# A state-space layer on one Trainium2 core: the first of two output products goes directly behind the projections, into another PSUM bank, and one column is copied ahead of the gating

## The chip, the cores and the metric

The kernel runs on one core of one Trainium2 chip. The metric is device time in microseconds (us) of one execution. Times of the kernel before: 1736.02, 1733.81 and 1731.57 us, median 1733.81.

## The reference

The input has 4 images of 128 channels and 96 x 96 pixels. The reference normalizes it in 32 groups of channels, reads it as four sequences of 9216 positions (rows forward, rows in reverse, columns forward, columns in reverse), runs the same scan layer on each, fuses the four results with a 1x1 convolution and adds the input. All is float32. The scan layer, cut to what matters here:

```python
t = _grouped1x1(x, in_proj_w, in_proj_b, G)
u, gate = (t[:, :HID], t[:, HID:])          # HID = 256
u = jax.nn.silu(u)
u = conv_general_dilated(u, dw_w, ..., feature_group_count=HID)   # 5 taps
s = _conv1x1(u, ssm_in_w)                   # 32 channels
a = DMIN + (DMAX - DMIN) * sigmoid(_conv1x1(u, ssm_delta_w, ssm_delta_b))
bb = tanh(_conv1x1(u, ssm_b_w, ssm_b_b))
cc = tanh(_conv1x1(u, ssm_c_w, ssm_c_b))
hst = ...                                   # h[l] = a[l] * h[l-1] + bb[l] * s[l]
u = u + _conv1x1(cc * hst + ssm_d[None, :, None] * s, ssm_out_w)
u = _grouped1x1(u * sigmoid(gate), mix_w, mix_b, G)
return _conv1x1(u, out_proj_w, out_proj_b)
```

## The kernel before, in words

**Tiling.** The program makes 8 passes over an image: for each of the 4 images one over columns (V) and one over rows (H). A pass takes the forward and the reverse sequence together. It has 6 steps of 4 *pairs*; a pair is one of four interleaved phases of a step, 384 positions of the forward unit (s = 0) and 384 of the reverse unit (s = 1). That makes 192 pairs, t = 0 to 191; k = t % 4 is the pair's place in its step. A helper `pair` issues the first 6 pairs, `pair_on` (L1038) those from t = 6 to 191, and `tail` the rest. The order of all instructions is the order in which the code issues them; no scheduler changes it. Each engine works through its own queue in order. In the text PE is the matrix engine, DVE the vector engine, ACT the scalar engine, POOL GpSimd, and SP the queue that issues transfers.

**A pair.** `pair_on(t)` does the front part of pair t and the back part of pair n = t - 6, whose recurrence is done by then. `bi` is the first unit of pair n. In the order of the code:

- *under(bi, 1)* (L659, the copy at L662): ACT copies u of the reverse unit into PSUM, two banks at a time, as the start value onto which ssm_out is added. The banks are given by `ssm`: 0 and 1 for the forward unit, 2 and 3 for the reverse one.
- *taps* (L814, L828): the upper half of the channels. The first tap is made by ACT a pair ahead (`first_tap`, L826); the four others are one DVE instruction each, the last writing u. They work in banks 0 and 1, which are also the forward unit's ssm_out banks.
- *band* (`conv`, L724): the lower half of the channels, 8 matmuls with a banded weight into banks 6 and 7. Phases k = 0 and 1 need a second part, *less* (`conv_less`, L784), and then ACT copies the banks into u (`copy_u`, L801); here these are called double pairs. In phases k = 2 and 3, the single pairs, DVE adds a row from the tile `lone` instead (`add_lone`, L775).
- *recurrence(t)* and *stats_chunks(t)*: DVE's scan (only k = 0 and 1), POOL's products for the scan's output, and in some pairs two blocks of statistics for the next image on DVE (L436).
- *first output product* (`add_next(w[0])`, `accumulate` at L931): 8 matmuls with the fused output weight w_fin on the gated u of the forward unit of pair n - 1, into bank 4. Then ACT copies the bank into ys (L946; L944 adds a bias in the last half of the H passes), and POOL adds ys to the output in SBUF (L963). The add is held back into the next pair where k = 3.
- *less* (double pairs), *under(bi, 0)*, *copy_u* (double pairs), and the *second output product* of the reverse unit into bank 5, again with a ys copy and a POOL add.
- *gates and ssm_out*: four matmuls for the gate of a later pair (L630) or the input projection of a later step (L492), into banks 4, 7, 6 and 5, mixed with the four matmuls of ssm_out (`out_of`, L650).
- *gating* (L700, the operation at L711): DVE multiplies ssm_out's result with the gate into u, in place, first the forward unit, then the reverse one. Between the two, the code hands ACT two activations on banks 4 and 5 (L505, L666 or L672).
- `first_tap(i + 2)` on ACT, then an activation on banks 6 and 7 (L516 or L672), and transfers.
- *proj* (L840): 16 matmuls of the projections with the weight `main` into banks 4 and 5; ACT's tanh tm (L865), copy (L868) and tanh (L874); POOL's start of the scan input; and `scale_s` (L886) on ACT.

A matmul of 128 x 32 weights fills a quarter of the array, so four of them run side by side. The trace has two MATMUL records for each float32 matmul.

**Waits.** An instruction waits for one semaphore itself. What else it waits for stands in separate wait instructions right ahead of it on the same engine.

## Time and profile before

| | |
|---|---|
| median of the three runs | 1733.81 us |
| the profiled execution's own time | 1736.02 us |
| its span, first to last instruction | 1734.3 us |
| matmuls (PE) busy | 1706.6 us |
| DVE busy | 1506.4 us |
| ACT busy | 1479.8 us |
| POOL busy | 1478.3 us |
| granted TensorE clock, mean | 0.998 |

The profile is one of the three runs. PE stands for matmuls and PEld for weight loads, which overlap them. In a timeline row the numbers are the start from the span's beginning and the length; rows of equal instructions that follow each other are merged, with their count. Brackets hold the idle time of the engine ahead of the row and what ended it. A line number can be that of a helper: L131 issues every matmul of proj, band, less and the output products, which are told apart by their weights (main, band, less, w_fin).

### The profile page before, as it was taken

Reading aid. Unit: us, or ns where it says so; the run is one execution under the profiler, and the core shown is the slowest. Engines: PE = TensorE matmul, PEld = TensorE weight load, DVE = VectorE, ACT = ScalarE, POOL = GpSimd, SP = SyncE. Lnnn points to the kernel's source line nnn. Section 1 sums busy time; section 2 is a strip of 40 time slices with the busy share of each in tenths; the row PEclk is TensorE's granted clock in tenths of the full one; section 3 lists DMA queues with packets and bytes.
Section 4 is the critical chain, followed back from the end, with each engine's and each line's share of the span. In section 5 each row is a group of like instructions: output and inputs, shape, how many; then the busy total and the mean of one; then the engine's idle time right before and its main releaser. Section 6 shows DMA issues by size and latency. Waiting matters only on the chain.

```text
span 1734.3 us, 50199 instructions
## 1 busy us (share of the span) xinstructions
PE 1706.6 (98%) x20410; PEld 703.5 (41%) x20410; DVE 1506.4 (87%) x1508; ACT 1479.8 (85%) x2435; POOL 1478.3 (85%) x1455
## 2 busy tenths in 40 slices
PE   7999999999999999999999999999999999999998
PEld 3343344434443434444444434444344433444333
DVE  6799998888889999888888989988888888888897
ACT  4788888888888888888888888888888888888875
POOL 3589898888889988988888988989888889998887
PEclk9999999999999999999999999999999999999999
DMA  7755885358994788337797488733899538753474
GB/s 241 208 169 163 281 242 146 131 197 261 287 289 152 232 245 246 124 132 251 238 306 232 154 275 239 216 117 126 253 287 288 192 119 275 227 167 116 132 239 169
DMA packets 143140, 362.63 MB, mean 209 GB/s; under 512 B 19264, under 2 KB 85696, under 8 KB 142912
## 3 DMA queue, kind: packets, MB, share of 16 engines
q1 hardware_dynamic: 142768, 359.39, 66.7%
q8 instruction: 162, 2.65, 0.7%
q14 instruction: 66, 0.54, 0.1%
q10 hardware_dynamic: 144, 0.04, 0.0%
HBM read 197.77 MB, written 126.70 MB: 187 GB/s over the span
## 4 chain that ended last, share of the span: by engine, by line
PE 89%; DMA 4%; DVE 3%; ACT 2%; issue 1%; POOL 0%; SPq 0%; ACTq 0%; DVEq 0%; POOLq 0%
PE psum L131 72%; PE psum L650 6%; PE psum L630 5%; PE psum L492 5%; DMA kept<-shared 2%; DVE psum L828 1%; DMA sil<-shared 1%; DMA sil<-sil 1%; DVE t L903 1%; DVE u L711 1%; ACT psum L826 1%; DMA acc<-in_xr 0%; PE psum L1274 0%; ACT psum L662 0%; ACT shared L516 0%
## 5 line engine op out<-in xcount | busy, mean ns | idle before, releaser
L828 DVE SCALAR_TENSOR_TENSOR psum<-sil,small,psum 128x768 f32<-128x768 f32 x576 | 589.2, 1023 | 51.6 <-ACT psum L826 34.0
L131 PE MATMUL psum<-u,w_fin 128*32 128x384 f32 (+1 forms) x6192 | 554.6, 485 | 1.1 <-ACT ys L944 0.5
L131 PE MATMUL psum<-u,main 128*32 128x384 f32 x6144 | 537.1, 490 | 1.2 <-ACT shared L672 0.6
L711 DVE SCALAR_TENSOR_TENSOR u<-gate,psum 128x768 f32<-128x768 f32 x376 | 341.9, 951 | 137.9 <-PE psum L650 65.0
L963 POOL TENSOR_TENSOR acc<-ys,acc 128x384 f32<-128x384 f32 x375 | 441.5, 1199 | 12.5 <-ACT ys L944 1.9
L131 PEld LDWEIGHTS psum<-u,w_fin 128*32 128x32 f32 x6192 | 203.1, 109 | 307.9 <-issue 209.3
L131 PEld LDWEIGHTS psum<-u,main 128*32 128x32 f32 x6144 | 180.2, 110 | 328.7 <-issue 207.3
L662 ACT COPY psum<-u 128x768 f32<-128x768 f32 x384 | 306.2, 798 | 7.1 <-DVE u L711 4.3
L909 POOL TENSOR_TENSOR t<-t,t 64x384 f32<-64x384 f32 (+1 forms) x192 | 261.8, 1364 | 45.6 <-DVE t L903 30.8
L131 PE MATMUL psum<-sil,band 128*32 128x384 f32 x3072 | 288.3, 486 | 4.4 <-ACT shared L516 2.2
L876 POOL TENSOR_SCALAR t<-tm 64x384 f32<-64x384 f32 x191 | 180.8, 947 | 125.3 <-ACT tm L865 113.4
L650 PE MATMUL psum<-t,main 32*128 32x384 f32 x1536 | 272.1, 519 | 3.7 <-ACT psum L662 3.0
L910 POOL TENSOR_TENSOR t<-t,t 64x384 f32<-64x384 f32 (+1 forms) x192 | 237.5, 1237 | 15.1
L877 POOL TENSOR_TENSOR t<-t,tm 64x384 f32<-64x384 f32 x192 | 235.6, 1227 | 15.3
L828 DVE SCALAR_TENSOR_TENSOR u<-sil,small,psum 128x768 f32<-128x768 f32 x192 | 194.9, 1015 | 6.8
L946 ACT COPY ys<-psum 128x384 f32<-128x384 f32 x288 | 138.3, 480 | 56.9 <-PE psum L131 46.9
L826 ACT ACTIVATE psum<-sil,small 128x768 f32<-128x768 f32 x191 | 171.7, 899 | 17.5 <-DVE u L711 13.4
L131 PEld LDWEIGHTS psum<-sil,band 128*32 128x32 f32 x3072 | 106.7, 109 | 153.2 <-issue 71.1
L630 PE MATMUL psum<-x_in,wn 32*128 32x384 f32 x768 | 161.0, 497 | 0.0
L492 PE MATMUL psum<-x_in,wn 32*128 32x385 f32 x704 | 149.4, 504 | 2.2 <-ACT sil L505 2.2
L505 ACT ACTIVATE sil<-psum,bnorm 128x385 f32<-128x385 f32 x176 | 102.4, 583 | 48.7 <-PE psum L492 35.5
L666 ACT ACTIVATE gate<-psum,bnorm 128x384 f32<-128x384 f32 x168 | 97.3, 581 | 43.5 <-PE psum L630 25.3
(112 smaller groups left out, 1692.6 us busy)
## 6 DMA issues: line engine op xcount, KB each, us to landing
gate<-kept SPq DMA_DIRECT2D x106, 768.0 KB, 5.6
kept<-gate SPq DMA_DIRECT2D x82, 768.0 KB, 3.7
sil<-sil SPq DMA_DIRECT2D x32, 770.0 KB, 7.9
sil<-shared SPq DMA_DIRECT2D x240, 96.2 KB, 2.8
x_in<-in_xs SPq DMA_DIRECT2D x194, 96.2 KB, 3.2
out<-acc SPq DMA_DIRECT2D x46, 384.0 KB, 7.7
x_in<-in_xs SPq DMA_DIRECT2D x88, 192.5 KB, 5.4
acc<-in_xr SPq DMA_DIRECT2D x39, 384.0 KB, 6.9
```

The lines of the kernel that those rows point to most:

```text
L131: nc.tensor.matmul(o[r, : rhs.shape[-1]], lhsT, rhs, start=start, stop=stop, skip_group_check=True)
L492: nc.tensor.matmul(bank(banks[2 * j + s])[:, : N + 1], stats[units[step * UB]["b"]][0][a, s, :], x_in[s][a, q, :], start=True, stop=True,)
L630: nc.tensor.matmul(bank(to)[:, :N], stats[un["b"]][0][r, s, :], x_in[s][r, q, off : off + N], start=True, stop=True)
L650: nc.tensor.matmul(bank(ssm(bi, s) + j)[:, :N], w_so[r, bass.ts(j, P)], z[r, :], start=(bi, s) not in seeded, stop=True, skip_group_check= ...
L662: nc.scalar.copy(psum[:, ssm(bi, s) : ssm(bi, s) + 2, :N], us[bi][:, s])
L711: nc.vector.scalar_tensor_tensor(v, g, 1.0, pz, ALU.add, ALU.mult)
L826: nc.scalar.activation(part, src, AF.Copy, scale=w_tap[:, 0:1])
L828: nc.vector.scalar_tensor_tensor(us[i][:, :, 1, :] if k == K - 1 else part, src, w_tap[:, k : k + 1], part, ALU.mult, ALU.add,)
L877: nc.gpsimd.tensor_mul(ta[0:64, p, :], tb[0:64, :], tm[0:64, :])
L909: engine.tensor_mul(ta[0:64, p, r], tb[64:P, r], ta[64:P, p, r])
L910: engine.tensor_add(tb[0:64, r], ta[0:64, p, r], tb[0:64, r])
L963: adder.tensor_add(part, y, part)
```

## The change

In `pair_on` the first output product moves ahead of under(bi, 1) in the code, and writes bank 2 in place of bank 4, except in the last pair (t = 191). Its POOL add stays where it was, by way of `settle`. The second product stays in bank 5. The other edit adds one DVE instruction ahead of the gating, which copies one column of the forward unit's u onto itself.

```diff
+        def add_next(bk):
+            return accumulate(waiting.pop(0), bk, *adder) if n else None
+
+        def settle(add):
+            if add:
+                held.append(add) if late or k == R - 1 and not last else add()
+
+        first = None if last else add_next(2)
         under(bi, 1)
...
-        def add_next(bk):
-            if n:
-                add = accumulate(waiting.pop(0), bk, *adder)
-                held.append(add) if late or k == R - 1 and not last else add()
-
-        add_next(w[0])
+        if last:
+            first = add_next(w[0])
+        settle(first)
         if not single:
             conv_less(i, banks, False)
         under(bi, 0)
         if not single:
             copy_u(i, banks)
-        add_next(w[1])
+        settle(add_next(w[1]))
...
         out_of(bi, 1, 0)
         gate_of(0, 1, 5)
         piece(t, 1)
+        corner = us[bi][:, 0, 0, 0:1]
+        nc.vector.tensor_copy(corner, corner)
         for s in range(2):
             gating(bi, s)
```

In what follows names carry numbers: u_2_3_2_0 is u of pass 2, step 3, phase 2, and the last number of a name counts buffers, so it differs between the kernels.

PE's queue from the end of the projections of a pair k = 1 (u_2_3_2_0) through the single pair behind it, with what each row waits for; before:

```order
L131 MATMUL psum_72<-u_2_3_2_0_5933,main_130 32x384 x7
L131 MATMUL psum_72<-sil_14_5053,band_142 32x384 [waits Activation_49]
L131 MATMUL psum_72<-sil_14_5053,band_142 32x384 x7
L131 MATMUL psum_72<-u_2_1_0_0_5388,w_fin_144 32x384 [waits DVE_49,Activation_49]
L131 MATMUL psum_72<-u_2_1_0_0_5388,w_fin_144 32x384 x7
L131 MATMUL psum_72<-u_2_1_0_0_5388,w_fin_144 32x384 [waits DVE_49,Activation_49]
L131 MATMUL psum_72<-u_2_1_0_0_5388,w_fin_144 32x384 x7
L630 MATMUL psum_72<-x_in1_71,wn_1_2480 128x384 [waits DMAHW1_49,Activation_49]
```

The same place in the changed kernel:

```order
L131 MATMUL psum_72<-u_2_3_2_0_5998,main_130 32x384 x7
L131 MATMUL psum_72<-u_2_1_0_0_5447,w_fin_144 32x384 [waits DVE_49]
L131 MATMUL psum_72<-u_2_1_0_0_5447,w_fin_144 32x384 x7
L131 MATMUL psum_72<-sil_14_5098,band_142 32x384 [waits Activation_49]
L131 MATMUL psum_72<-sil_14_5098,band_142 32x384 x7
L131 MATMUL psum_72<-u_2_1_0_0_5447,w_fin_144 32x384 [waits Activation_49]
L131 MATMUL psum_72<-u_2_1_0_0_5447,w_fin_144 32x384 x7
L630 MATMUL psum_72<-x_in1_71,wn_1_2498 128x384 [waits DMAHW1_49]
```

The first product now stands ahead of the band and waits for DVE alone (the second gating, which reads bank 2); the second product and the first gate matmul wait for one engine less.

ACT's queue in the same pair, from the last tanh of proj to the second ys; before:

```order
L874 ACTIVATE t1_2_3_2_0_5997<-psum_72,small_91 64x384
L886 ACTIVATE t1_2_3_1_0_5908<-t1_2_3_1_0_5908,small_91 64x384 [waits Activation_49]
L662 COPY psum_72<-u_2_2_1_0_5474 128x2x384 [waits DVE_49]
L946 COPY ys_2_1_0_0_6051<-psum_72 128x384 [waits PE_49]
L662 COPY psum_72<-u_2_2_1_0_5474 128x2x384 [waits DVE_49]
L946 COPY ys_2_1_0_1_6063<-psum_72 128x384 [waits PE_49]
```

And in the changed kernel:

```order
L874 ACTIVATE t1_2_3_2_0_6053<-psum_72,small_91 64x384
L886 ACTIVATE t1_2_3_1_0_5963<-t1_2_3_1_0_5963,small_91 64x384
L946 COPY ys_2_1_0_0_6085<-psum_72 128x384 [waits DVE_49,PE_49]
L662 COPY psum_72<-u_2_2_1_0_5534 128x2x384 [waits Activation_49]
L662 COPY psum_72<-u_2_2_1_0_5534 128x2x384 [waits DVE_49]
L946 COPY ys_2_1_0_1_6119<-psum_72 128x384 [waits PE_49]
```

The first ys copy and under(bi, 1) have changed places. The wait of the latter for ACT is a wait for the ys copy right ahead of it, since both use bank 2.

DVE's queue from the last tap of that pair to the gating; before:

```order
L828 SCALAR_TENSOR_TENSOR u_2_3_3_0_6022<-sil_14_5053,small_91,psum_72 128x2x384 [waits DVE_49]
L775 SCALAR_TENSOR_TENSOR u_2_3_3_0_6022<-shared_5054,small_91,psum_72 128x2x384 [waits PE_49,Activation_49]
L436 BN_STATS bn_2_5311<-xs_2_8_5770 128x6 [waits DMAHW5_49]
L436 BN_STATS bn_2_5311<-xs_2_9_5772 128x6 [waits DMAHW6_49]
L711 SCALAR_TENSOR_TENSOR u_2_2_1_0_5474<-gate0_176,psum_72 128x768 [waits PE_49,Activation_49]
L711 SCALAR_TENSOR_TENSOR u_2_2_1_0_5474<-gate0_176,psum_72 128x768 [waits PE_49]
```

And in the changed kernel:

```order
L828 SCALAR_TENSOR_TENSOR u_2_3_3_0_6088<-sil_14_5098,small_91,psum_72 128x2x384 [waits DVE_49]
L775 SCALAR_TENSOR_TENSOR u_2_3_3_0_6088<-shared_5099,small_91,psum_72 128x2x384 [waits PE_49,Activation_49]
L436 BN_STATS bn_2_5369<-xs_2_8_5833 128x6 [waits DMAHW5_49]
L436 BN_STATS bn_2_5369<-xs_2_9_5835 128x6 [waits DMAHW6_49]
L1122 COPY u_2_2_1_0_5534<-u_2_2_1_0_5534 128x1 [waits Activation_49]
L711 SCALAR_TENSOR_TENSOR u_2_2_1_0_5534<-gate0_176,psum_72 128x768 [waits DVE_49,PE_49]
L711 SCALAR_TENSOR_TENSOR u_2_2_1_0_5534<-gate0_176,psum_72 128x768 [waits PE_49]
```

The copy (L1122) takes over the wait for ACT (for under(bi, 0), which reads the u that the gating overwrites). The first gating waits for the copy and for PE.

## Prediction

> **What bounds the kernel now.** I read the page first: how busy TensorE is, and the chain that ended last.
>
> ```profile
> PE 1706.6 (98%) x20410; PEld 703.5 (41%) x20410; DVE 1506.4 (87%) x1508; ACT 1479.8 (85%) x2435; POOL 1478.3 (85%) x1455
> PE 89%; DMA 4%; DVE 3%; ACT 2%; issue 1%; POOL 0%; SPq 0%; ACTq 0%; DVEq 0%; POOLq 0%
> ```
>
> TensorE is busy for 98% and makes up 89% of the chain, so the change can only win back small gaps between matmuls. The next question is where they are. I took the timeline of two pairs that follow each other, first the end of a double pair (its band is in two parts) and then a whole single pair (t = 90, k = 2). Columns: start, length, engine, operation; in brackets the idle time before it and its releaser.
>
> ```profile
> 803.69 0.13 PEld L131 LDWEIGHTS psum<-u,w_fin 128*32 128x32 f32 x4 [0.19 <-issue]
> 804.01 0.13 PEld L131 LDWEIGHTS psum<-u,w_fin 128*32 128x32 f32 x4 [0.19 <-issue]
> ...
> 807.32 0.58 PE L630 MATMUL psum<-x_in,wn 32*128 32x384 f32 x1
> 807.33 0.60 PE L650 MATMUL psum<-t,main 32*128 32x384 f32 x3
> ...
> 808.43 1.82 DVE L711 SCALAR_TENSOR_TENSOR u<-gate,psum 128x768 f32<-128x768 f32 x2 [0.45 <-PE psum L650]
> ...
> 808.90 2.79 PE L131 MATMUL psum<-u,main 128*32 128x384 f32 x32
> ...
> 810.41 3.14 DVE L828 SCALAR_TENSOR_TENSOR psum<-sil,small,psum 128x768 f32<-128x768 f32 x3 [0.16 <-ACT psum L826]
> ...
> 811.51 1.48 PE L131 MATMUL psum<-sil,band 128*32 128x384 f32 x16
> ...
> 812.80 2.76 PE L131 MATMUL psum<-u,w_fin 128*32 128x384 f32 x32
> ...
> 812.86 0.62 ACT L886 ACTIVATE t<-t,small 64x384 f32<-64x384 f32 x1
> ...
> 813.38 0.79 ACT L662 COPY psum<-u 128x768 f32<-128x768 f32 x1
> ...
> 813.58 1.01 DVE L828 SCALAR_TENSOR_TENSOR u<-sil,small,psum 128x768 f32<-128x768 f32 x1
> ...
> 814.34 0.48 ACT L946 COPY ys<-psum 128x384 f32<-128x384 f32 x1 [0.17 <-PE psum L131]
> ...
> 814.72 0.81 ACT L662 COPY psum<-u 128x768 f32<-128x768 f32 x1
> ...
> 815.49 0.58 PE L630 MATMUL psum<-x_in,wn 32*128 32x384 f32 x1
> ...
> 815.67 0.60 PE L650 MATMUL psum<-t,main 32*128 32x384 f32 x3
> ...
> 816.69 1.82 DVE L711 SCALAR_TENSOR_TENSOR u<-gate,psum 128x768 f32<-128x768 f32 x2 [1.17 <-ACT ys L946]
> ...
> 817.16 2.79 PE L131 MATMUL psum<-u,main 128*32 128x384 f32 x32
> 817.32 0.58 ACT L672 ACTIVATE shared<-psum,bnorm 128x384 f32<-128x384 f32 x1 [0.30 <-PE psum L630]
> 817.80 0.90 ACT L826 ACTIVATE psum<-sil,small 128x768 f32<-128x768 f32 x1
> ```
>
> In the double pair the first ssm_out matmul (L650) starts 0.01 us behind the first gate matmul (L630). In the single pair it starts 0.18 behind it: TensorE waits for under(0), the L662 copy that starts at 814.72. From the first gate matmul to the next projections it takes 817.16 - 815.49 = 1.67 us in the single pair and 808.90 - 807.32 = 1.58 in the double one. So a single pair has about 0.09 us of TensorE time to give, and a double pair nothing at this place. The single pair is a cycle of waits: DVE's last tap (ends 814.59), under(0) on ACT, ssm_out on PE, gating on DVE, first tap, taps. Its period from gating to gating is 816.69 - 808.43 = 8.26 us.
>
> Why does under(0) start at 814.72, 0.13 behind the last tap? On ACT's queue the ys copy of the first product stands ahead of it. That copy waits for PE (0.17 idle), since the product runs only behind the band: with as many matmuls as the band's row, which takes 1.48, it ends at about 812.80 + 1.48 = 814.28. The copy ends at 814.82, and under(0) starts 0.10 before that end, as neighbours on ACT do here when none waits for the other (L662 at 813.38 starts 0.10 before L886's end, 813.48).
>
> **The change, part by part.** Its own time is 1736.02 us for a span of 1734.3; that run is the slowest of the three, 2.2 over their median. I sum changes and apply them to the median, 1733.81.
>
> *First product ahead of the band, single pairs.* The projections need 811.51 - 808.90 = 2.61 us up to the next group, the band 812.80 - 811.51 = 1.29, a product the same. The product now ends at about 811.51 + 1.48 = 812.99, before ACT is done with L886 (813.48), so ys waits for nothing on PE. New is that under(1) writes the bank that ys reads and waits for it. ACT's queue: ys 813.38 to 813.86, under(1) 0.04 behind its end, 813.90 to 814.69, under(0) from 814.59. Now the tap is last: 814.59 + 0.04 = 814.63 against 814.72, a gain of 0.09. The 0.04 is what a wait for the instruction just ahead costs on DVE: three taps take 3.14 us in a row where one takes 1.023 (below), so (3.14 - 3 x 1.023) / 2.
>
> What is late next in other single pairs? Here are the rows of a k = 3 pair with a plain ys copy and of one with a ys that adds a bias (L944), each from a timeline:
>
> ```profile
> 505.89 0.62 ACT L886 ACTIVATE t<-t,small 64x384 f32<-64x384 f32 x1
> ...
> 506.68 1.01 DVE L828 SCALAR_TENSOR_TENSOR u<-sil,small,psum 128x768 f32<-128x768 f32 x1
> 507.37 0.48 ACT L946 COPY ys<-psum 128x384 f32<-128x384 f32 x1 [0.17 <-PE psum L131]
> ...
> 507.74 0.81 ACT L662 COPY psum<-u 128x768 f32<-128x768 f32 x1
> ```
> ```profile
> 821.12 0.62 ACT L886 ACTIVATE t<-t,small 64x384 f32<-64x384 f32 x1
> ...
> 821.90 1.01 DVE L828 SCALAR_TENSOR_TENSOR u<-sil,small,psum 128x768 f32<-128x768 f32 x1
> 822.60 0.59 ACT L944 ACTIVATE ys<-psum,b_fin 128x384 f32<-128x384 f32 x1 [0.17 <-PE psum L131]
> ...
> 823.08 0.81 ACT L662 COPY psum<-u 128x768 f32<-128x768 f32 x1
> ```
>
> In the first, the tap ends at 507.69 and under(0) starts at 507.74: DVE is nearly last already, and 0.02 is left. In the second, ys could start at 821.64, under(1) at 822.27 and under(0) at 822.96, against 823.08: 0.12. The biased form makes 87 of some 370 ys copies, two in each pair with products:
>
> ```profile
> L944 ACT ACTIVATE ys<-psum,b_fin 128x384 f32<-128x384 f32 x87 | 50.5, 582 | 14.4 <-PE psum L131 12.8 <-POOL t L876 0.5
> ```
>
> So k = 3 gains 0.77 x 0.02 + 0.23 x 0.12 = 0.04 a pair. The product goes into another place from pair 7 to 190, which is 46 pairs of each k: 46 x 0.09 + 46 x 0.04 = 6.0 us.
>
> *Band behind the product.* The band waits for banks 6 and 7 to be read by ACT (L672 or L516). Where ACT is late there, the product now fills the time. PE's waits of this kind, in all, count and longest:
>
> ```profile
> PE psum L131 <- ACT shared L672: 2.6, 4, 1.3
> PE psum L131 <- ACT shared L516: 2.2, 6, 1.0
> ```
>
> One of them in a double pair, with its projections:
>
> ```profile
> 624.64 2.79 PE L131 MATMUL psum<-u,main 128*32 128x384 f32 x32
> ...
> 627.72 1.50 PE L131 MATMUL psum<-sil,band 128*32 128x384 f32 x16 [0.29 <-ACT shared L516]
> ```
>
> The band starts 3.08 behind the projections instead of 2.61, so 0.47 is lost where the row shows 0.29 idle. The other 0.18 is hidden because groups start 0.32 apart (803.69, 804.01) while a record is longer. All ten would give 4.8 + 10 x 0.18 = 6.6 us; that is the upper bound. The Trainium skill, Perfetto Trace Analysis, section Identifying the Most-Contended Engine, says that matmul busy share is no good measure, since pipelined matmuls overlap; the trace agrees (0.47 against 0.29), and by idle time alone this bound would be 4.8. I do not take 6.6. In single pairs the late ACT makes under(0) late as well, and PE then waits there instead. In double pairs ACT's copies behind the late one stay where they are, and gates need them, so I take half: of the L516 row without its longest, (2.2 - 1.0 + 5 x 0.18) / 2 = 1.0 us.
>
> *What the product waits for.* It must not overwrite bank 2 before the second gating has read it: 808.43 + 1.82 = 810.25, and the product comes at 811.51, so 1.2 us of cover; its cost is nothing up to that. Behind a product that waits, band, less and second product would be queued. DVE's add of the lone row (L775) needs the band, which now ends 1.29 later, at 811.51 + 1.48 + 1.29 = 814.28; DVE is busy with the tap until 814.59. Zero, with 0.3 to spare. The second product's bank and place, POOL's additions and SP's queue keep their order.
>
> *The copied column.* It takes the wait for ACT off the gating, which then waits for PE itself. Nearest rows for its price and cover, from the groups of DVE's instructions (time in all, mean in ns, idle time before them) and from a timeline:
>
> ```profile
> L828 DVE SCALAR_TENSOR_TENSOR psum<-sil,small,psum 128x768 f32<-128x768 f32 x576 | 589.2, 1023 | 51.6 <-ACT psum L826 34.0 <-ACT sil L600 0.8
> L711 DVE SCALAR_TENSOR_TENSOR u<-gate,psum 128x768 f32<-128x768 f32 x376 | 341.9, 951 | 137.9 <-PE psum L650 65.0 <-ACT ys L944 31.6 <-ACT ys L946 30.8
> ...
> L243 DVE COPY mean<-psum 128x1 f32<-128x1 f32 x3 | 0.5, 152 | 0.0
> ```
> ```profile
> 508.53 1.01 DVE L436 BATCH_NORM_STATS2 bn<-xs 128x6 f32<-128x384 f32 x2
> ...
> 509.71 1.82 DVE L711 SCALAR_TENSOR_TENSOR u<-gate,psum 128x768 f32<-128x768 f32 x2 [0.17 <-issue]
> ```
>
> It costs 0.152 + 0.04 = 0.19 us, 186 times, 35 us of DVE if nothing covered it. DVE idles 137.9 us before 188 first gatings, 0.73 each, so it is covered, except in the pairs with two statistics blocks (0.17 left), where it is 0.02 too long. The Trainium skill, VectorE: DVE Perf Modes, section The TRN2 errata, speaks against small operations: each pays a fixed cost, by its formula about 59 cycles at 0.96 GHz or 0.06 us (an estimate); the row says 0.152, and by the page the bound would be 186 x 0.10 = 19 us. The gain is between 0 and one hop between semaphores, some 0.05 us. I take 0, since the gating is not what the next pair waits for: at 816.69 it needs 0.95 for its first half, to 817.64, but the first tap starts at 817.80, behind ACT's second tanh of 817.32, which follows PE's gate matmuls.
>
> **Sum:** 6.0 + 1.0 + 0 = 7 us, 0.4%: 1733.8 - 7 = 1727 us.
>
> **The rivals.** *DVE is last at once (about 1731).* If the last tap comes as late in k = 2 as in the plain k = 3 pair, every single pair gains 0.02: 92 x 0.02 + 1.0 = 3 us. For it: the k = 3 rows. Against it: 0.13 between tap and copy in the k = 2 rows.
>
> *Everything is won (about 1719).* Single pairs fall to the 1.58 of double ones, 92 x 0.09 = 8.3, and all ten waits go, 6.6: 15 us. Against it: the tap's end at 507.69, and ACT late for the gates.
>
> *ACT becomes the late one (about 1740).* If ys, with its extra wait for DVE, and under(0) lose their 0.10 overlaps, the k = 2 queue reads ys 813.48 to 813.96, under(1) 814.00 to 814.79, under(0) 814.79: 0.07 later than now. The plain k = 3 pair: 506.51, 507.03, 507.82 against 507.74: 0.08 later. 92 x 0.075 - 1.0 = +6 us. It decides once under(0) starts over 0.13 behind the tap. For it: under(1) now waits for its neighbour. Against it: neither ys nor under(0) waits for its neighbour.
>
> **How the numbers follow.** The forecast has 0.50 (own range 1723 to 1731), DVE last 0.28, everything won 0.12, ACT late 0.10. The range 1719 to 1737 holds the first two with a spread of 2 us between runs on either side (1731.57 to 1736.02), and half of the third; what it leaves out is under 0.2. A measurement here can tell 0.3%, 5.2 us, from no change. Faster than that are 0.40 of the forecast and 0.12: 0.52. Within it are 0.10 of the forecast and 0.28: 0.38. Slower is 0.10.
>
> **What would show it.** In a k = 2 pair of the changed profile: projections, product, band in steps of 2.61 and 1.29; ys right behind L886 with no PE wait; under(0) within 0.06 of the last tap's end; the first ssm_out matmul at most 0.1 behind the first gate matmul; gating to gating near 8.18. The L672 and L516 rows of PE's waits should be gone and the copied column should take about 0.15 us. I am wrong if under(0) starts over 0.13 behind the tap, if PE's first product waits for the gating, or if single pairs shrink and double pairs grow.

## The result and the profile after

The changed kernel takes 1746.29 us (median of 6 runs, 1743.75 to 1749.62), the kernel before, timed beside it, 1736.04 us (6 runs, 1731.57 to 1738.46): ratio 1.0065, 95% interval 1.0051 to 1.0079. It is slower by 0.65%, some 11 us, where the prediction said 7 us faster, and it lies outside the range of 1719 to 1737. The profiled execution took 1749.62 us for a span of 1748.0.

First the page of the changed kernel: busy time of each engine, and the chain that ended last.

```profile
PE 1719.4 (98%) x20410; PEld 685.3 (39%) x20410; DVE 1545.8 (88%) x1694; ACT 1500.0 (86%) x2435; POOL 1455.1 (83%) x1455
PE 88%; DMA 5%; POOL 2%; ACT 2%; DVE 1%; issue 1%; SPq 0%; POOLq 0%; DVEq 0%; ACTq 0%
```

DVE has 186 instructions more, as it should. They account for 186 x 0.149 = 27.8 us, but DVE is busy for 39 us more. So something else on DVE got longer too. PE is busy for 13 us more, although it does the same work: the mean record of an output product is as long as before (488 ns, 487 before), but records that run side by side count once, and here they overlap less.

Now the single pair that the prediction followed, t = 90, in the timeline of the changed kernel (start, length, engine, operation, idle time before it):

```profile
815.37 2.79 PE L131 MATMUL psum<-u,main 128*32 128x384 f32 x32
...
817.98 1.47 PE L131 MATMUL psum<-u,w_fin 128*32 128x384 f32 x16
...
819.27 1.48 PE L131 MATMUL psum<-sil,band 128*32 128x384 f32 x16
819.33 0.62 ACT L886 ACTIVATE t<-t,small 64x384 f32<-64x384 f32 x1
819.97 0.48 ACT L946 COPY ys<-psum 128x384 f32<-128x384 f32 x1
820.05 1.01 DVE L828 SCALAR_TENSOR_TENSOR u<-sil,small,psum 128x768 f32<-128x768 f32 x1
820.48 1.53 ACT L662 COPY psum<-u 128x768 f32<-128x768 f32 x2
...
821.96 0.58 PE L630 MATMUL psum<-x_in,wn 32*128 32x384 f32 x1
...
822.16 0.60 PE L650 MATMUL psum<-t,main 32*128 32x384 f32 x3
```

The order is the intended one: product 2.61 behind the projections' start, band 1.29 behind that, ys right behind L886 (0.02) with no wait for PE. But the first ssm_out matmul starts 0.20 behind the first gate matmul, where it was 0.18. The two L662 copies are one row here: the second ends at 822.01 and takes 0.80 as in the kernel before, so under(0) starts at 821.21, 0.15 behind the last tap's end (821.06). Before, it was 0.13.

This pair hardly changed. To see which pairs did, I took the period of every pair from the trace, from the first projection matmul of the pair ahead of it to its own, since the projections end a pair. The table has the median period by k, and the sum over the 46 pairs of each k (t = 7 to 190) as a difference from the kernel before. The medians of k = 1 to 3 repeat from run to run within 0.01 us where nothing was edited; pairs k = 0 are of two kinds, near 9.11 and from 9.25 up, and their median jumps between the two. The sums also hold the waits for transfers, which differ between executions by some us.

| kernel | k = 0 | k = 1 | k = 2 | k = 3 | sums, k = 0, 1, 2, 3 |
|---|---|---|---|---|---|
| before | 9.250 | 9.131 | 8.261 | 8.262 | |
| changed | 9.113 | 9.136 | 8.433 | 8.286 | -2.9, +0.8, +10.7, +3.4 |

Of the 46 double pairs k = 0, 22 got shorter, by 0.13 to 0.46 and by 4.9 us in all, and nearly all the others did not change. In 20 of the 22 the band's first record starts on time in the kernel before, 2.58 to 2.60 behind the projections, and its last one 3.73 to 4.06 behind them, where 3.59 is usual; with the product ahead, the band always takes its usual time. ACT has read the banks at least 0.24 ahead of that start in both kinds of pairs, so this is not the wait for ACT that the prediction counted. Where I compared the two kinds (t = 56 and 76 against t = 60), PE's queue has more waits between the band's first matmuls; what these wait for I did not follow. The loss lies in single pairs, above all in k = 2, and only in some of them: of the 46, 19 are longer by 0.43 to 0.52, most of the others by 0.02 to 0.16. Here is what stands ahead of one of these, the end of t = 60 (k = 0) to the end of t = 61 (k = 1) and the gates of t = 62 (k = 2), on DVE and around it. The kernel before:

```profile
550.87 3.13 DVE L903 TENSOR_TENSOR_SCAN t<-t,t 64x768 f32<-64x768 f32 x1
...
554.03 1.82 DVE L711 SCALAR_TENSOR_TENSOR u<-gate,psum 128x768 f32<-128x768 f32 x2
...
560.18 1.81 DVE L903 TENSOR_TENSOR_SCAN t<-t 64x768 f32<-64x768 f32 x1
...
560.47 2.33 POOL L877 TENSOR_TENSOR t<-t,tm 64x384 f32<-64x384 f32 x1
...
562.86 1.82 DVE L711 SCALAR_TENSOR_TENSOR u<-gate,psum 128x768 f32<-128x768 f32 x2 [0.86 <-PE psum L650]
...
563.34 2.79 PE L131 MATMUL psum<-u,main 128*32 128x384 f32 x32
...
569.93 0.58 PE L630 MATMUL psum<-x_in,wn 32*128 32x384 f32 x1
...
570.10 0.60 PE L650 MATMUL psum<-t,main 32*128 32x384 f32 x3
```

The changed kernel:

```profile
554.01 3.13 DVE L903 TENSOR_TENSOR_SCAN t<-t,t 64x768 f32<-64x768 f32 x1
...
557.24 0.15 DVE L1122 COPY u<-u 128x1 f32<-128x1 f32 x1
557.51 1.82 DVE L711 SCALAR_TENSOR_TENSOR u<-gate,psum 128x768 f32<-128x768 f32 x2
...
563.59 1.01 POOL L877 TENSOR_TENSOR t<-t,tm 64x384 f32<-64x384 f32 x1
563.66 2.55 DVE L903 TENSOR_TENSOR_SCAN t<-t 64x768 f32<-64x768 f32 x1
...
566.32 0.15 DVE L1122 COPY u<-u 128x1 f32<-128x1 f32 x1
...
566.46 2.79 PE L131 MATMUL psum<-u,main 128*32 128x384 f32 x32
...
566.58 1.82 DVE L711 SCALAR_TENSOR_TENSOR u<-gate,psum 128x768 f32<-128x768 f32 x2
...
567.57 0.91 ACT L826 ACTIVATE psum<-sil,small 128x768 f32<-128x768 f32 x1 [0.42 <-DVE u L711]
...
573.05 0.91 PE L630 MATMUL psum<-x_in,wn 32*128 32x384 f32 x2
...
573.68 0.94 PE L650 MATMUL psum<-t,main 32*128 32x384 f32 x8
```

Read it in four steps. (1) In the kernel before, the gating of k = 0 starts 0.03 behind the end of the scan (550.87 + 3.13 = 554.00): DVE has no idle time there. With the column the gating starts 557.51 - 557.14 = 0.37 behind it, 0.34 later. (2) The taps of k = 1 therefore end 0.34 later, and the scan of k = 1 now starts 0.07 behind POOL's product L877 and not 0.29 ahead of it. It takes 2.55 instead of 1.81: 0.74 more. (3) Behind it the column costs 0.37 again. (4) Against this stands the gating's wait for PE of 0.86 in the kernel before. 0.34 + 0.74 + 0.37 - 0.86 = 0.59 us too much. Measured against the projections, the gating moved from 0.48 ahead (562.86, 563.34) to 0.12 behind (566.58, 566.46): 0.60. The first tap of the next pair now waits for the gating, the taps are late, under(0) too, and in t = 62 the first ssm_out matmul stands 0.63 behind the first gate matmul instead of 0.17.

The other pairs bear this out. In 21 pairs k = 1 the scan changed sides, from 1.81 to between 2.53 and 2.64, and the 21 pairs k = 2 behind them are longer by 0.30 to 0.82, 10.1 us of the 10.7. Of the other 25 only one is longer by more than 0.2. The 21 stand behind the 21 pairs k = 0 whose gating had the least idle time ahead of it in the kernel before: 0.03 in 17 of them, 0.06 to 0.17 in four. In 16 of the other 25 the scan had started behind L877 in the kernel before already, so it had no place left to lose.

In the waits of ACT the first tap's wait for the gating is a row of its own (sum, count, longest), before and after:

```profile
ACT psum L826 <- DVE u L711: 13.4, 17, 1.7
```
```profile
ACT psum L826 <- DVE u L711: 34.0, 53, 2.5
PE psum L131 <- ACT shared L672: 1.3, 2, 0.7
PE psum L131 <- DVE u L711: 1.4, 1, 1.4
```

It stood in the profile before already, 17 times. Of the ten PE waits for L672 and L516 two are left, and one product did wait for the gating.

### The profile page after: what moved, and what is told of

Its sections match the earlier page's. It is cut to its first block, busy times and chain, and to the rows that moved or that the text cites. A ratio compares the mean times of both kernels' runs of the same rounds, so it can differ in the third digit from the quotient of the medians.

```text
span 1748.0 us, 50159 instructions
## 1 busy us (share of the span) xinstructions
PE 1719.4 (98%) x20410; PEld 685.3 (39%) x20410; DVE 1545.8 (88%) x1694; ACT 1500.0 (86%) x2435; POOL 1455.1 (83%) x1455
## 3 DMA queue, kind: packets, MB, share of 16 engines
q8 instruction: 161, 2.64, 0.6%
## 4 chain that ended last, share of the span: by engine, by line
PE 88%; DMA 5%; POOL 2%; ACT 2%; DVE 1%; issue 1%; SPq 0%; POOLq 0%; DVEq 0%; ACTq 0%
PE psum L131 70%; PE psum L650 7%; PE psum L630 5%; PE psum L492 5%; DMA sil<-sil 3%; DMA acc<-in_xr 1%; POOL acc L963 1%; DMA sil<-front 1%; DMA gate<-kept 1%; POOL t L909 0%; DMA kept<-shared 0%; ACT psum L662 0%; POOL t L877 0%; DVE psum L828 0%; POOL t L910 0%
## 5 line engine op out<-in xcount | busy, mean ns | idle before, releaser
L131 PE MATMUL psum<-u,w_fin 128*32 128x384 f32 (+1 forms) x6192 | 567.2, 485 | 2.3 <-DVE u L711 1.4
L131 PEld LDWEIGHTS psum<-u,w_fin 128*32 128x32 f32 x6192 | 190.5, 109 | 321.9 <-issue 251.3
L662 ACT COPY psum<-u 128x768 f32<-128x768 f32 x384 | 298.0, 801 | 13.7 <-DVE u L711 4.3
L876 POOL TENSOR_SCALAR t<-tm 64x384 f32<-64x384 f32 x191 | 181.7, 951 | 131.2 <-ACT tm L865 119.5
L131 PE MATMUL psum<-sil,band 128*32 128x384 f32 x3072 | 283.4, 486 | 0.0
L650 PE MATMUL psum<-t,main 32*128 32x384 f32 x1536 | 258.8, 520 | 4.8 <-ACT psum L662 3.2
L877 POOL TENSOR_TENSOR t<-t,tm 64x384 f32<-64x384 f32 x192 | 211.5, 1101 | 15.3
L131 PEld LDWEIGHTS psum<-sil,band 128*32 128x32 f32 x3072 | 99.3, 110 | 149.8 <-issue 115.9
```

Of the source, the lines that this page charges most:

```text
L131: nc.tensor.matmul(o[r, : rhs.shape[-1]], lhsT, rhs, start=start, stop=stop, skip_group_check=True)
L650: nc.tensor.matmul(bank(ssm(bi, s) + j)[:, :N], w_so[r, bass.ts(j, P)], z[r, :], start=(bi, s) not in seeded, stop=True, skip_group_check= ...
L662: nc.scalar.copy(psum[:, ssm(bi, s) : ssm(bi, s) + 2, :N], us[bi][:, s])
L876: nc.gpsimd.tensor_scalar(*decay(i))
L877: nc.gpsimd.tensor_mul(ta[0:64, p, :], tb[0:64, :], tm[0:64, :])
```

## The experiments

Two theories stood at the start. *The column*: it stands behind the scan in DVE's queue, and double pairs pass the delay on. *The order*: product, ys and POOL's add come earlier and collide with the scan; the column has no part in it. Ratios are to the kernel before on the same chip, with 95% intervals. One thousandth is 1.7 us.

### One part alone

Without the column (e1), with the column alone (e2), with the column in single pairs alone (e3), and with two columns (e4):

```diff
 e1, changed kernel:
-        corner = us[bi][:, 0, 0, 0:1]
-        nc.vector.tensor_copy(corner, corner)
 e2, kernel before:
         piece(t, 1)
+        corner = us[bi][:, 0, 0, 0:1]
+        nc.vector.tensor_copy(corner, corner)
 e3, changed kernel:
+        if single:
             corner = us[bi][:, 0, 0, 0:1]
             nc.vector.tensor_copy(corner, corner)
 e4, changed kernel:
+        for e in range(2):
+            corner = us[bi][:, 0, 0, e : e + 1]
             nc.vector.tensor_copy(corner, corner)
```

> The changed kernel without the copied column; the first product stays ahead of the band, in bank 2. Theory (column): the column stands in VectorE's queue behind the scan and ahead of the gating; in pairs k = 0 and 1 this makes the gating late, and the pair after pays. Without it the 6 to 7 us of the order of the products are left: 1727 to 1731 us, and the first ssm_out matmul of k = 2 pairs starts about 0.1 behind the first gate matmul, not 0.4. Rival (order): product, ys copy and what POOL adds come earlier, and collide with the scan; the column has no part in it: 1744 to 1748 us, as the changed kernel, and still 0.4 in k = 2.

> The kernel before with the copied column alone; the products stay where they were. Theory (column): 1742 to 1756 us, since the loss is the column's and nothing is won; first ssm_out matmul of k = 2 pairs later than before by 0.2 to 0.3 in the mean. Rival (order): 1734 to 1738 us, as before.

> The changed kernel with the copied column in single pairs (k = 2 and 3) alone, where no scan stands ahead of it. Theory (column behind the scan): no loss, as without the column or up to 5 us better, since the gating of single pairs loses a hop of about 0.06: 1724 to 1731 us. Rival (order): 1744 to 1748 us. If the column costs the same wherever it stands, half of the loss is left: about 1737 us.

> The changed kernel with two copied columns, one behind the other, in every pair. Theory (column): VectorE's gating is later by another 0.2 us in pairs k = 0 and 1, and since those pairs are late already, the pair after pays most of it: 1753 to 1765 us. Rival (order): 1745 to 1750 us, no more than the changed kernel.

| kernel | median us | ratio | k = 0 | k = 1 | k = 2 | k = 3 | sums |
|---|---|---|---|---|---|---|---|
| e1 order alone | 1738.51 | 1.0019 (1.0004 to 1.0035) | 9.113 | 9.116 | 8.286 | 8.286 | -5.1, -1.2, +0.8, +5.7 |
| e2 column alone | 1739.55 | 1.0030 (1.0018 to 1.0041) | 9.143 | 9.204 | 8.354 | 8.263 | -0.5, +4.8, +3.8, -3.7 |
| e3 order, column in single pairs | 1735.77 | 1.0010 (0.9998 to 1.0022) | 9.113 | 9.116 | 8.285 | 8.287 | -5.6, -1.4, +0.3, +3.1 |
| e4 order, two columns | 1746.44 | 1.0073 (1.0052 to 1.0094) | 9.114 | 9.188 | 8.451 | 8.284 | -3.9, +2.1, +10.7, +4.2 |

Both theories are half right, and e2 lies between the ranges that the two had given it. The column in double pairs is most of the loss: 1.0065 with it (changed kernel) and 1.0010 without (e3), and the sum of k = 2 falls from +10.7 to +0.3. Where no scan stands ahead of it, it costs nothing. But the order alone is no gain either, it is 0.19% slower; the 1727 to 1731 us that the first theory gave e1 were wrong. And a second column costs next to nothing: e4 was expected at 1753 us at least, and took 1746.44. In t = 60 of e4 the second column starts 0.07 behind the first, and the gating 0.43 behind the scan's end, not 0.37: a second one adds 0.06, since most of the 0.37 is the waiting between scan, column and gating.

### The order by pairs

The order in double pairs alone (e5) and in single pairs alone (e6), both without the column:

```diff
 changed kernel without the column; e5 (e6 has "not single" in its place):
-        first = None if last else add_next(2)
+        stay = last or single
+        first = None if stay else add_next(2)
...
-        if last:
+        if stay:
             first = add_next(w[0])
```

> No copied column; the first product goes ahead of the band in double pairs (k = 0 and 1) alone, single pairs are as before. Theory (ACT late in single pairs): the order by itself wins some 5 us in double pairs, where the product fills waits for banks 6 and 7, and loses it in single pairs, where ys and under(1) stand close behind each other and under(0) starts 0.03 later: 1727 to 1731 us, 3 to 6 below the kernel before. Rival (as predicted: single pairs win, double pairs little): 1732 to 1734 us.

> No copied column; the first product goes ahead of the band in single pairs (k = 2 and 3) alone. Theory (ACT late in single pairs): 92 x 0.024 = 2 us of loss in the regular pairs and up to 5 more in the pairs with statistics blocks: 1736 to 1741 us. Rival (single pairs win): 1727 to 1731 us.

| kernel | median us | ratio | k = 0 | k = 1 | k = 2 | k = 3 | sums |
|---|---|---|---|---|---|---|---|
| e5 double pairs | 1734.70 | 1.0008 (0.9989 to 1.0027) | 9.114 | 9.116 | 8.262 | 8.263 | -2.2, -0.8, +0.3, +1.3 |
| e6 single pairs | 1741.26 | 1.0043 (1.0025 to 1.0061) | 9.142 | 9.141 | 8.285 | 8.287 | +0.9, -0.2, +2.0, +6.0 |

In single pairs, where the prediction had its 6 us, the order loses. The regular part is 8.286 - 8.261 = 0.024 a pair, 92 x 0.024 = 2.2 us. It comes from ACT's queue, as the timeline of e1 shows for t = 90 (projections at 809.89):

```profile
813.85 0.61 ACT L886 ACTIVATE t<-t,small 64x384 f32<-64x384 f32 x1
...
814.49 0.48 ACT L946 COPY ys<-psum 128x384 f32<-128x384 f32 x1
814.57 1.01 DVE L828 SCALAR_TENSOR_TENSOR u<-sil,small,psum 128x768 f32<-128x768 f32 x1
815.00 1.53 ACT L662 COPY psum<-u 128x768 f32<-128x768 f32 x2
```

ys starts 0.03 behind the end of L886, where under(1) used to start 0.10 ahead of it; under(1) starts 0.03 behind ys; under(0) starts at 816.53 - 0.80 = 815.73, 0.15 behind the tap's end (815.58). The rest of e6's loss is in k = 3, at one place of each pass, where ACT's L672 waits until a transfer has read its tile:

```profile
ACT shared L672 <- DMA kept<-shared: 9.1, 9, 1.9
```

That is e1. The row's sum is 4.9 to 9.7 us in each of the eight kernels that have the order in single pairs, and 3.3 at most in nine of the other ten, the kernel before among them (7.5 in the tenth, e16 below). Why these transfers land later is open: I did not follow it. In double pairs e5 shows the shorter pairs k = 0 (22 of them, 4.7 us in all), but not in its time, against the 3 to 6 us that I expected: waits in other pairs k = 0 take 2.5 us of it back. The parts also don't add up: e5 and e6 give 1.0051 together, and e1, from an earlier batch of runs, has 1.0019; the intervals overlap, and why they differ is open.

### Which double pair, and the collision

The column in k = 0 alone on the kernel before (e7); on the changed kernel without the column in k = 0 (e14) or in k = 1 (e15); and the changed kernel with POOL's product L877 of two tiles replaced, in the projections of k = 0, by an operation on one (e8, which leaves out a factor of the scan's input in a quarter of the pairs):

```diff
 e7, kernel before:
+        if k == 0:
+            corner = us[bi][:, 0, 0, 0:1]
+            nc.vector.tensor_copy(corner, corner)
 e14, changed kernel (e15: k != 1):
+        if k != 0:
             corner = us[bi][:, 0, 0, 0:1]
             nc.vector.tensor_copy(corner, corner)
 e8, changed kernel:
-        nc.gpsimd.tensor_mul(ta[0:64, p, :], tb[0:64, :], tm[0:64, :])
+        if i // 2 % R or i < 2 * LAG:
+            nc.gpsimd.tensor_mul(ta[0:64, p, :], tb[0:64, :], tm[0:64, :])
+        else:
+            nc.gpsimd.tensor_scalar(ta[0:64, p, :], tb[0:64, :], 1.0, None, ALU.mult)
```

> The kernel before with the copied column in pairs k = 0 alone. Theory (the column makes the gating late behind the scan of k = 0, all taps of k = 1 come later, and the scan of k = 1 then starts behind POOL's product L877 instead of ahead of it): the scans of k = 1 take 2.3 to 2.4 us in the mean, not 2.0, and most of the loss of the column in all pairs is here: 1737 to 1740 us. Rival (each pair pays its own column): scans stay at 2.0 and a quarter to a half of that loss, 1735 to 1736 us.

> The changed kernel, but POOL's product of two tiles (L877) in the projections of pairs k = 0 is an operation of the same size on one tile, so that half of the scan's second operand lacks a factor there. Theory (VectorE's scan and a POOL operation on two tiles hold each other up): scans of k = 1 back at 1.81 us in nearly all pairs, gating and taps of k = 2 earlier, first ssm_out matmul of k = 2 pairs 0.2 instead of 0.4 behind the first gate matmul: 1736 to 1741 us. Rival (the column's queue time alone makes k = 2 late): 1744 to 1748 us, whatever the scans take.

> The changed kernel without the column in pairs k = 0 (k = 1, 2, 3 keep it). The budget: in the pair t = 61 of the kernel before, the gating of k = 1 waits 0.86 us for PE behind the scan; in the changed kernel the scan starts 0.34 later, is 0.74 longer and the column adds 0.37 behind it, 1.45 in all, 0.59 too much. Without the column of k = 0 only the 0.37 are left: no loss in k = 2, scans of k = 1 at 2.0 to 2.1, 1734 to 1738 us. Rival (each column costs its share): half of the loss stays, 1740 to 1742 us.

> The changed kernel without the column in pairs k = 1 (k = 0, 2, 3 keep it). By the budget 0.34 + 0.74 - 0.86 = 0.22 too much is left: scans of k = 1 still 2.3 to 2.4, the pairs k = 2 that lost 0.45 lose 0.1 to 0.2, 1737 to 1741 us. Rival (the column of k = 1 is the whole loss): as without any column, 1734 to 1738 us, and no pair k = 2 longer than without it.

The last column is the mean of a group of 56 scans, the 48 of k = 1 and the first of each pass.

| kernel | median us | ratio | k = 1 | k = 2 | sums | scans, us |
|---|---|---|---|---|---|---|
| before | | | 9.131 | 8.261 | | 2.082 |
| changed | 1746.29 | 1.0065 (1.0051 to 1.0079) | 9.136 | 8.433 | -2.9, +0.8, +10.7, +3.4 | 2.385 |
| e7 column in k = 0 alone | 1738.28 | 1.0021 (1.0004 to 1.0039) | 9.204 | 8.261 | -1.0, +5.6, -1.4, -2.0 | 2.363 |
| e8 other POOL operation | 1737.25 | 1.0021 (1.0004 to 1.0038) | 9.139 | 8.287 | -5.3, +1.0, +0.9, +3.4 | 2.071 |
| e14 no column in k = 0 | 1737.16 | 1.0017 (1.0006 to 1.0029) | 9.117 | 8.285 | -3.2, -0.9, +1.5, +3.5 | 2.112 |
| e15 no column in k = 1 | 1741.47 | 1.0034 (1.0021 to 1.0048) | 9.139 | 8.383 | -1.9, +0.7, +4.9, +6.2 | 2.389 |

The rows of the groups, kernel before and changed kernel:

```profile
L903 DVE TENSOR_TENSOR_SCAN t<-t 64x768 f32<-64x768 f32 x56 | 116.6, 2082 | 1.8
```
```profile
L903 DVE TENSOR_TENSOR_SCAN t<-t 64x768 f32<-64x768 f32 x56 | 133.6, 2385 | 1.8
```

The budget holds. Take away the column of k = 0 (e14): the scans are short again, the column of k = 1 fits into the 0.86, and nothing is left of the loss but the order's own (e1: 1.0019). Take away the column of k = 1 (e15): the scans stay long, 0.34 + 0.74 - 0.86 = 0.22 is too much, and the affected k = 2 pairs lose 0.10 to 0.21, mostly, instead of 0.45. Take away the collision alone and leave both columns in place (e8): 0.34 + 0.22 + 0.37 - 0.86 = 0.07 is too much, the sum of k = 2 falls from +10.7 to +0.9 (e1 has +0.8) and the ratio from 1.0065 to 1.0021, near e1's 1.0019. In e8 the scans did not come down to 1.81, as I had expected, but to about 2.03; t = 61 shows it:

```profile
560.05 1.58 POOL L880 TENSOR_SCALAR t<-t 64x384 f32<-64x384 f32 x1
560.13 2.03 DVE L906 TENSOR_TENSOR_SCAN t<-t 64x768 f32<-64x768 f32 x1
```

e7 came out at the time expected and for another reason. Its scans are long, as in the changed kernel, but k = 2 loses nothing. The loss is one pair earlier, in k = 1, in its timeline of t = 61:

```profile
554.08 0.15 DVE L1118 COPY u<-u 128x1 f32<-128x1 f32 x1
...
557.11 1.50 PE L131 MATMUL psum<-sil,band 128*32 128x384 f32 x16 [0.15 <-ACT gate L672]
...
560.41 1.01 POOL L877 TENSOR_TENSOR t<-t,tm 64x384 f32<-64x384 f32 x1
560.49 2.54 DVE L903 TENSOR_TENSOR_SCAN t<-t 64x768 f32<-64x768 f32 x1
...
563.17 1.82 DVE L711 SCALAR_TENSOR_TENSOR u<-gate,psum 128x768 f32<-128x768 f32 x2
...
563.64 2.79 PE L131 MATMUL psum<-u,main 128*32 128x384 f32 x32
```

The late gating of k = 0 makes ACT's first tap and L672 late, and the band, still the first group there, waits for its banks: it starts 2.94 behind the projections, not 2.61. So the two parts of the change meet here: with the product ahead of the band this wait is covered, and the delay goes on to the scan and to k = 2. A long scan without a column behind it does no harm: the gating is 0.47 ahead of the projections, as before.

Next, a delay of VectorE by itself, on the kernel before: two copies of a spare column ahead of the scan in k = 1 (e10), or at the same place in k = 2, where no scan follows (e11).

```diff
...
+        if k == 1:        # e11: k == 2
+            for _ in range(2):
+                nc.vector.tensor_copy(spare, spare)
         recurrence(t)
```

> The kernel before with two copies of one column of a spare tile on VectorE right ahead of the scan in pairs k = 1; they wait for nobody and nobody for them. Theory (scan and POOL's product L877 hold each other up, and who starts first is decided by 0.3 us): the scans start some 0.3 later, behind L877, and take 2.3 to 2.6 us in the mean instead of 2.0; 1738 to 1742 us. Rival (VectorE's queue time alone counts): scans stay at 2.0, under 1737 us.

> The same two copies at the same place in pairs k = 2, where no scan stands behind them. Theory (collision): VectorE has 1.17 idle before the gating there, so nothing happens: 1733 to 1736 us, scans as before. Rival (any 0.3 us on VectorE costs the same): 1738 to 1742 us.

e10 took 1734.03 us, ratio 0.9991 (0.9981 to 1.0002), e11 1732.59, ratio 0.9986 (0.9973 to 0.9998). In e10 the group of scans went from 2.082 to 2.204, but no time was lost: my expectation was wrong, and the rival's "under 1737" is what happened, though scans did not stay at 2.0. The two copies delay the scan by only 0.22 to 0.24, and 10 scans change sides, not 21. The budget still holds for them: in t = 61 the scan takes 2.67, and 0.24 + 0.86 is 0.24 over the gating's 0.86; six of the 46 pairs k = 2 were longer, by 0.10 to 0.12. e11's medians are those of the kernel before (8.262 in k = 2); I know no reason for its 0.14%. So a ratio that is 0.15 to 0.2% off, as those of e1, e8, e14 and e13, is weak evidence by itself; the periods of the pairs carry the argument there.

### An earlier ys without the shared bank

If under(1)'s place behind ys is what spoils single pairs, the first product should keep bank 4 and still come earlier. It can stand inside the band. On the kernel before, in single pairs, with the first six of the band's eight groups ahead of it (e9) or four, one bank's worth (e13). `conv` takes the range of groups that it issues; `add_next` and `settle` are those of the changed kernel:

```diff
...
+        split = single and not last
+        if split:
+            conv(i, banks, True, range(6))        # e13: range(4)
+            first = add_next(w[0])
+            conv(i, banks, True, range(6, 8))     # e13: range(4, 8)
+        else:
             conv(i, banks, single)
...
-        add_next(w[0])
+        settle(first if split else add_next(w[0]))
```

> The kernel before; in single pairs the first product keeps its own bank 4 and stands between the first six and the last two groups of the band, and its ys copy stays behind under(1). So ys comes 0.3 us earlier and under(1) waits for nothing new. Theory (in single pairs the failed step is under(1), which waits for ys when the product is in bank 2): under(0) starts 0.03 to 0.06 behind the last tap in k = 2, not 0.12 as before or 0.16 with bank 2; k = 2 pairs shrink by 0.08, k = 3 by 0.02: 46 x 0.08 + 46 x 0.02 = 5 us, 1728 to 1731 us. Rival (an earlier ys brings nothing, since the cycle of VectorE, ACT and PE gives it back elsewhere): as before, 1733 to 1736 us.

> The kernel before; in single pairs the first product, in its own bank 4, stands between the band's first four groups (one bank) and its last four (the other bank). Now all of the product ends about 0.6 us earlier, and ys follows under(1) with no PE wait. Theory (under(1)'s wait for ys is the failed step): under(0) starts 0.03 to 0.06 behind the last tap, first ssm_out matmul 0.08 to 0.1 behind the first gate matmul, single pairs of k = 2 shrink by 0.06 to 0.08 and of k = 3 by 0.02: 1728 to 1732 us, ratio near 0.998. Rival (an earlier ys brings nothing in the cycle of VectorE, ACT and PE): 0.9995 to 1.0005.

e9 took 1734.26 us, ratio 0.9997 (0.9984 to 1.0011), with the period of every kind of pair as before. But it had tried nothing, as its t = 90 shows (projections at 808.06):

```profile
810.67 1.14 PE L131 MATMUL psum<-sil,band 128*32 128x384 f32 x10
811.33 0.52 PE L131 MATMUL psum<-u,w_fin 128*32 128x384 f32 x2
811.64 0.49 PE L131 MATMUL psum<-sil,band 128*32 128x384 f32 x2
...
812.93 0.49 PE L131 MATMUL psum<-u,w_fin 128*32 128x384 f32 x2
...
813.50 0.48 ACT L945 COPY ys<-psum 128x384 f32<-128x384 f32 x1 [0.17 <-PE psum L131]
```

Records of band and product alternate here, and the product's last matmuls start at 812.93, 4.87 behind the projections. ys comes no earlier, 5.44 behind them as in the kernel before. I read this as both running side by side, each in the quarters of the array that the other leaves free. Split by banks (e13), the whole product stands between the two halves of the band, from 3.25 behind the projections to 4.72. e13 took 1731.45 us, ratio 0.9978 (0.9965 to 0.9991), faster than the kernel before. Its t = 90 (projections at 807.24):

```profile
811.71 0.79 ACT L662 COPY psum<-u 128x768 f32<-128x768 f32 x1
...
811.91 1.01 DVE L827 SCALAR_TENSOR_TENSOR u<-sil,small,psum 128x768 f32<-128x768 f32 x1
...
812.52 0.48 ACT L945 COPY ys<-psum 128x384 f32<-128x384 f32 x1
...
812.96 0.80 ACT L662 COPY psum<-u 128x768 f32<-128x768 f32 x1
...
813.82 0.58 PE L630 MATMUL psum<-x_in,wn 32*128 32x384 f32 x1
...
813.91 0.60 PE L650 MATMUL psum<-t,main 32*128 32x384 f32 x3
```

under(0) starts 0.04 behind the tap's end (812.92) and ssm_out 0.09 behind the first gate matmul. The medians are 9.247, 9.123, 8.170 and 8.239: k = 2 gains 0.09 (0.09 or more in 42 of the 46 pairs) and k = 3 0.02, which is what the prediction wanted from the changed order. The rival, that the cycle gives it back elsewhere, is out.

Last, e13's single pairs with the changed kernel's order in double pairs (e16), and e9's with them (e12):

```diff
 e12 and e16, on e9 and e13:
+        split, stay = single and not last, single or last
+        first = None if stay else add_next(2)
         under(bi, 1)
...
-        settle(first if split else add_next(w[0]))
+        settle(first if split or not stay else add_next(w[0]))
```

> Single pairs as in the split band, double pairs with the first product ahead of the band in bank 2, no copied column. If both parts win what their places show (5 us in single pairs, 0 to 4 in double ones): 1725 to 1731 us. If the double pairs' order brings nothing, as the split band alone.

> Single pairs with the band in halves and the first product between them (bank 4), double pairs with the first product ahead of the band in bank 2, no copied column. If the shorter pairs k = 0 count (2 to 4 us), 1727 to 1730 us, ratio 0.995 to 0.997; if waits for transfers eat them, as the halved band alone: ratio 0.997 to 0.999.

e12: 1734.05 us, ratio 1.0002 (0.9988 to 1.0015). e16: 1732.73 us, ratio 0.9989 (0.9973 to 1.0006). The median of k = 0 is 0.14 lower in both (9.114 and 9.113), and the time shows nothing of it. In e16's profile k = 3 is 3.6 us longer in all, and L672's wait for the transfer is back at 7.5 us. So e13 is the best version found, 0.22% below the kernel before, though its interval and e16's overlap; whether the double pairs' order could be had as well is open.

## Why the prediction was wrong, step by step

**What bounds the kernel.** The cycle of single pairs, with under(0) 0.13 behind the tap, was read rightly, and the size of what it can give too: e13 wins 0.09 in k = 2 and 0.02 in k = 3, 46 x 0.09 + 46 x 0.02 = 5 us of the 6.0 that the term had.

**First product ahead of the band, single pairs (6.0 us): wrong sign, 2.2 us lost.** The failed step is "ACT's queue: ys 813.38 to 813.86, under(1) 0.04 behind its end, 813.90 to 814.69, under(0) from 814.59". Counted from the projections' start (808.90 there, 815.37 in the changed kernel) it put ys at 4.48, under(1) at 5.00, under(0) at 5.69. Measured: 4.60, 5.11, 5.84. under(1)'s wait of 0.03 was right. What failed is the overlap: ys does not start 0.10 ahead of L886's end but 0.02 behind it, and under(0) starts 0.06 ahead of under(1)'s end, not 0.10. Neither is chance: in the whole trace ys stands 0.02 behind L886 in each of 184 places, where under(1) stood 0.09 to 0.10 ahead of its end in the kernel before. That is the third rival's mechanism (ACT becomes the late one, chance 0.10, from 0.13 behind the tap; it is 0.15), at a third of its price of 0.07 to 0.08 (0.024 a pair): the first of its two overlaps is lost, the second mostly kept. The argument against it, that ys does not wait for its neighbour, was no argument: a neighbour that is not waited for can still start late. Why ys and under(1) differ there was not tried.

**Band behind product (1.0 us): the cover right, what it covers in part missed, the gain unproven in the time.** Eight of ten waits for ACT are gone, as said. But 22 pairs k = 0 are shorter by 4.9 us in all, and in 20 of them the band did not wait for ACT: its later matmuls were late by 0.14 to 0.47, which the prediction had no term for. That the sum stays under the upper bound of 6.6 is luck. e5 and e16 show no gain in time beside it (1.0008, and 0.9989 against e13's 0.9978).

**What the product waits for (0): nearly right.** One product waited, 1.4 us, in t = 100, where the gating was late itself; that is one of the signs of being wrong that the prediction named. The cover of 1.2 is down to 569.07 - (566.58 + 1.82) = 0.67 in t = 62. The add of the lone row cost nothing, as said.

**The copied column (0): the step that cost most, some 9 us.** Its length was right (0.15). "DVE idles 137.9 us before 188 first gatings, 0.73 each, so it is covered" is the failed step: a mean over pairs with very different cover. In 17 of the 46 pairs k = 0 the idle time is 0.03, and the cost there is not 0.19 but 0.34 (0.11 on either side of it and 0.15 itself, less the 0.03). "The gating is not what the next pair waits for" fails in double pairs; the row of ACT's waits for it, 17 times, stood in the profile before. And the price was not the column alone: 0.34 made a scan of 1.81 one of 2.55 (2.53 to 2.64 in 21 pairs), which no bound of the prediction held. The third rival's time, 1740, was nearest, but for a smaller reason.

**The sum.** Order alone +0.19%, 3.3 us; column in double pairs 1.0065 - 1.0010, some 9.5 us; column in single pairs (e3 against e1) not to be told from nothing. Together 0.65%, and -7 had been said. Of the marks named, 2.61 and 1.29, ys right behind L886 and the column's 0.15 were right; under(0) within 0.06, ssm_out at most 0.1 behind and 8.18 from gating to gating were not.

## What to carry to other kernels

Idle time ahead of an instruction is cover only in the kind of loop turn where it stands; look it up in the tightest one, behind whatever is queued there, before a mean is used. Delays add up against one cover, and a small one can turn the order of two engines that hold each other up: write the budget of the turn (here 0.34 + 0.74 + 0.37 against 0.86) and not the price of the instruction. An earlier result is worth nothing if its bank makes the next copy wait in the queue; to bring it forward, check in the trace that the work put behind it really starts behind it (e13), and does not run beside it (e9).

## What the runs showed of the hardware

- A scan on VectorE with two operands in SBUF and a POOL product of two tiles hold each other up. The scan takes 1.81 when it starts first and 2.55 when the product has started 0.07 earlier and has 0.94 to go; the product takes 1.01 when it comes first, and 2.33 when the scan has started 0.29 earlier and has 1.52 to go. The edge is sharp: of all scans and products in the traces here that start within 0.12 of each other, the scan takes 1.81 whenever it starts 0.051 or more ahead, and 2.50 or more whenever its lead is 0.046 or less. The Trainium skill, SBUF — State Buffer, section Who interferes with whom, says that a VectorE instruction with two SBUF inputs contends with a POOL instruction that reads SBUF, that the lock on the port is exclusive, and that the order of issue decides who blocks. These rows agree, but for 0.20: if the later one did nothing until the other's end, it would take 0.94 + 1.81 = 2.75 and 1.52 + 1.01 = 2.53. With an operation on one tile in place of the product the trace differs: the scan loses 0.22 while 1.50 of the operation is left, and the operation takes 1.58 where another of that kind and size (L876) takes 0.92, so both slow down.
- A copy of one column of 128 x 1 takes 0.15 us on VectorE, and 0.34 to 0.37 of the queue between two instructions that it depends on or that depend on it.
- Matmuls with 128 x 32 weights in different quarters of the array start out of the code's order (e9: twelve records of the band stand ahead of the first product in the code, and two of them start at 811.64, behind two of the product's at 811.33).
